# Four graph neural network layers on one core: the lags of the attention jobs in a planner's order of priorities, for the last graphs

## The chip, the cores and the metric

The kernel runs on one core of a Trainium2 chip. The metric is the device time of one execution in microseconds (us). The core's engines are named as in the profile: PE (TensorE, matmuls), PEld (its weight loads), DVE (VectorE), ACT (ScalarE), POOL (GpSimd) and SP (SyncE, which here only issues DMAs).

## The reference

There are 16 graphs of 1024 nodes with 128 features each; `adj` holds one 1024 x 1024 matrix of zeros and ones per graph. Four layers follow one another, each on the layernorm and relu of x and with x added to its result:

```python
h = relu(layernorm(x)); x = x + sage3(h, dilate(adj), ...)      # layer 0: three convolutions, batch norms over all graphs
h = relu(layernorm(x)); x = x + attention(h, adj, ...)          # layer 1
h = relu(layernorm(x)); x = x + gat(h, adj, W, a)               # layer 2
h = relu(layernorm(x)); x = x + gcn(h, adj, W, b)               # layer 3
# layer 1: 4 heads of 32; softmax(q k^T * 32**-0.5 + log(max(adj, 1e-8))) @ v, then @ Wo.T + bo
# layer 2: e[i,j] = leaky_relu(s_i[i] + s_j[j], 0.2) where adj > 1e-8; softmax over i, 4 heads; alpha^T @ (h @ W)
# layer 3: D^-1/2 (adj + I) D^-1/2 h @ W.T + b,   D = row sums of adj + I
```

Layer 0 needs statistics over all graphs. Layers 1 to 3 need only their own graph, so graph 5 can be in layer 3 while graph 7 is in layer 1.

## The kernel before

`whole` runs layer 0 first (`dilate_plain`, `convolutions_plain`, up to about 1580 us of the profile) and then `attentions_plain`, in which the change lies. This function does layers 1 to 3 of all graphs in one stretch. It consists of seven generators, the jobs, each of which loops over the 16 graphs:

- `matrices` brings the rows of A (fp8) of a graph, checks that A is symmetric (L1318 to L1335: ACT, DVE, PE), and ends with `dinv` (DVE L1338, POOL L1340). Only then is `A[b]` there for the others.
- `before` finishes layer 0 for a graph (L1365), makes the norm (L1265 to L1282, output `h_a`), q, k and v.
- `attend` makes 16 tiles per graph: ACT writes a scaled piece of A over a PSUM tile of four banks (L1416, out `t`), PE adds k^T q to it (L1421, eight matmuls), ACT takes two exponentials (L1429, out `e`). There is one PSUM tile and there are two `e` buffers, so tile n waits until `values` has used tile n - 2.
- `values` multiplies each `e` with v and with ones (L1452), divides (L1458, L1460), multiplies with Wo (L1303) and adds to x (L1462). With that the attention of the graph is complete.
- `positive` makes the masks of layer 2 on DVE (L1503, 32 a graph, out `pm`), from scores that go through DRAM (`dst<-scores`).
- `gat` is the rest of layer 2: norm (output `h`), the product with W (L1523), the split in three bf16 parts (L1549 to L1555), sums with A (L1563) and with the masks (L1578), and the closing operations on POOL and DVE (L1587 to L1598).
- `gcn` is layer 3: norm (output `h_g`), parts (L1615 to L1621), the product with A (L1632, L1636), the product with W (L1303), the last additions on POOL (L1610, L1644), and the store.

A job's generator works on one graph at a time, so gat of graph 15 can't begin ahead of the end of gat of graph 14. `matrices` and `before` of graph b wait until gcn of graph b - 4 and the attention of graph b - 2 are done (four buffers for A and x). Jobs other than `attend` and `values` share two PSUM banks, the pool "sum".

No engine chooses at run time: every engine gets one list of instructions, in the order in which the planner `in_order` lets the generators go on. Each `yield` announces the next operation: engine, planned duration, the planned time from which its inputs are there, and the change in PSUM banks. The planner takes the job with the smallest key, gives it its operation and a planned end, and goes on. The key has three parts:

```python
start = max([free[engine], needs] + [min(pools[pool]) for pool, change in tiles(j) if change > 0])
key = (start, engine == "PE", j["did"] / j["per"] + j["lag"])
```

`did` is the planned PE time that the job has had so far and `per` a number from the list at L1649, so `did / per` is a progress, roughly in graphs. A small key is a high priority. The planned durations are constants, and the chip's differ from them. The planner is also used at L921, for layer 0, with lags that are plain numbers.

Of the kernel before, what the change touches and what calls it, by code (L numbers as in the profile page):

```python
# [1213 lines left out]
def attentions_plain(tc, x, spill, final, ready_weights, adj, deg, trouble, eye, out, scores, bound, reach):  # L1214
    nc = tc.nc
    with ExitStack() as ctx:
# [26 lines left out]
        def bank(pool=psg, name="sum"):  # L1243
            return pool.tile([P, HN], F32, name=name)
# [63 lines left out]
        def matrices():  # L1308

            for b in range(B):  # L1310
                while done["gcn"] < b - 3 or done["attend"] < b - 1:
                    yield
                m = adp.tile([P, NB, N], F8, name="A")
                for i in range(NB):
                    t = yield "ACT", 1.3, 0.0, 0
                    a = lp.tile([P, N], F32, name="a")
                    nc.sync.dma_start(a, adj[b, i * P:(i + 1) * P, :])
                    nc.scalar.activation(m[:, i, :], a, AF.Relu, accum_out=deg[:, b, i:i + 1], saturate=False)  # L1318
                    yield "DVE", 1.4, 0.0, 0
                    junk = lp.tile([P, N], F8, name="junk", bufs=1)  # L1320

                    nc.vector.scalar_tensor_tensor(junk, a, 0.0, a, op0=ALU.is_gt, op1=ALU.not_equal,
                                                   accum_out=trouble[:, b, i, 0:1], saturate=False)
                    for hf in range(2):
                        w = min(HN, (i - 4 * hf) * P)
                        if w > 0:
                            e = yield "PE", 0.1 + w / 1024, t, 1
                            ps = bank()
                            nc.tensor.matmul(ps[:, :w], ident16, m[:, i, hf * HN:hf * HN + w], start=True, stop=False)
                            for j in range(w // P):  # L1330
                                nc.tensor.matmul(ps[:, j * P:(j + 1) * P], m[:, 4 * hf + j, i * P:(i + 1) * P], minus16,
                                                 start=False, stop=j == w // P - 1)
                            yield "ACT", 0.8, e, -1
                            junk = lp.tile([P, HN], BF16, name="junk2", bufs=1)
                            nc.scalar.activation(junk[:, :w], ps[:, :w], AF.Abs, accum_out=trouble[:, b, i, 1 + hf:2 + hf])  # L1335

                t = yield "DVE", 0.2, 0.0, 0
                nc.vector.tensor_scalar(dinv[:, b], deg[:, b], 1.0, None, op0=ALU.add)  # L1338
                yield "POOL", 1.7, t, 0
                nc.gpsimd.tensor_tensor(dinv[:, b], dinv[:, b], minus_half, op=ALU.pow)  # L1340
                A[b] = m
# [55 lines left out]
        def attend():  # L1397

            last = 0.0


            s = pss.tile([P, H, HN], F32, name="t")
            for hd in range(H):
                for c in range(4):
                    nc.tensor.matmul(s[:, hd, c * P:(c + 1) * P], ident16, ident16, start=c == 0, stop=c == 3)
            n = 0
            for b in range(B):
                while b not in ready or b not in A:
                    yield
                t, xt, qT, kT, va = ready[b]  # L1410
                for hf in range(2):
                    cols = slice(hf * HN, (hf + 1) * HN)
                    for k in range(NB):
                        e = yield "ACT", 1.9, last, 0

                        nc.scalar.activation(s, A[b][:, k, None, cols].to_broadcast([P, H, HN]), AF.Copy, scale=16.0)  # L1416
                        e = yield "PE", 1.1, max(e, t), 0

                        for hd in range(H):
                            r = slice(hd * HD, (hd + 1) * HD)  # L1420
                            nc.tensor.matmul(s[:, hd], kT[r, k * P:(k + 1) * P], qT[r, cols], start=False, stop=True,  # L1421
                                             skip_group_check=True)
                        while n > 1 and n - 2 not in taken:
                            yield
                        es = ep.tile([P, H, HN], F32, name="e")
                        e = max(e, taken.get(n - 2, 0.0))
                        for hd in range(0, H, 2):
                            e = yield "ACT", 1.07, e, 0
                            nc.scalar.activation(es[:, hd:hd + 2], s[:, hd:hd + 2], AF.Exp, scale=SIGMA)  # L1429
                        exps[n] = es, e  # L1430
                        last = e
                        n += 1
# [213 lines left out]
                done["gcn"] += 1  # L1646

        with tc.manual_schedule(engines=set(ENGINES.values())):
            in_order([(0, 4.0, matrices()), (3, 18.0, before()), (0.5, 17.6, attend()), (3, 34.0, values()), (1, 2.0, positive()),  # L1649
                      (1, 54.0, gat()), (2.5, 17.0, gcn())], {"sum": 2})  # L1650


ENGINES = {"PE": mybir.EngineType.PE, "ACT": mybir.EngineType.Activation, "DVE": mybir.EngineType.DVE,
           "POOL": mybir.EngineType.Pool}
HOP = 0.25


def in_order(jobs, pools):

    free = dict.fromkeys(ENGINES, 0.0)
    pools = {name: [0.0] * n for name, n in pools.items()}
    first = next(iter(pools))
    jobs = [{"lag": lag, "per": per, "job": job, "next": next(job), "held": {}, "did": 0.0, "asked": False}
            for lag, per, job in jobs]

    def tiles(j):  # L1670
        bank = j["next"][3]
        return bank if isinstance(bank, list) else [bank if isinstance(bank, tuple) else (first, bank)]

    while True:
        best = None
        for j in jobs:
            while j["next"] is None and not j["asked"]:
                j["next"], j["asked"] = next(j["job"], "end"), True
            if j["next"] in (None, "end"):
                continue  # L1680
            engine, took, needs, _ = j["next"]
            start = max([free[engine], needs] + [min(pools[pool]) for pool, change in tiles(j) if change > 0])
            key = (start, engine == "PE", j["did"] / j["per"] + j["lag"])
            if best is None or key < best[0]:
                best = (key, start, j)
        jobs = [j for j in jobs if j["next"] != "end"]
        if best is None:
            assert not jobs
            break
        _, start, j = best  # L1690
        assert start < float("inf")
        engine, took, needs, _ = j["next"]
        end = free[engine] = start + took
        if engine == "PE":
            j["did"] += took
        for pool, change in tiles(j):
            if change > 0:
                k = pools[pool].index(min(pools[pool]))
                pools[pool][k] = float("inf")
                j["held"].setdefault(pool, []).append(k)  # L1700
            elif change < 0:
                pools[pool][j["held"][pool].pop(0)] = end + HOP
        try:
            j["next"] = j["job"].send(end + HOP)
        except StopIteration:
            jobs.remove(j)
        for o in jobs:
            o["asked"] = False
# [39 lines left out]
def whole(tc, x, adj, nodemask, chunk_mats, chunk_mask, eye, sel, p, out):  # L1748
    nc = tc.nc
    with tc.tile_pool(name="dram", bufs=1, space=DRAM) as dp, tc.tile_pool(name="keep", bufs=1) as kp:  # L1750
# [19 lines left out]
        with tc.tile_pool(name="final", bufs=1) as fp:  # L1770
            final = [fp.tile([P, D], F32, name=f"final{i}") for i in range(3)] + [fp.tile([3, D], BF16, name="final_row")]
            with tc.tile_pool(name="early", bufs=1) as yp, tc.tile_pool(name="c_adj", bufs=2) as ap, \
                    tc.tile_pool(name="c_x", bufs=2) as xp:
                ident = yp.tile([P, P], F32, name="ident")
                nc.sync.dma_start(ident, eye)
                minus_half = yp.tile([P, NB], F32, name="minus_half")
                nc.vector.memset(minus_half, -0.5)
                h0 = xp.tile([P, NB, D], F32, name="xt")
                attention_weights(tc, ap, ident, ready_weights, *weights)
                dilate_plain(tc, adj, eye, kept, rdeg, unsettled, norm_first(tc, x, yp, h0, minus_half))  # L1780
                convolutions_plain(tc, x, ident, ap, xp, h0, minus_half, kept, rdeg, spill, final, *layer0)
            attentions_plain(tc, x, spill, final, ready_weights, adj, deg, trouble, eye, out, scores, bound, reach)
# [45 lines left out]
```

## Time and profile before

| | |
|---|---|
| time, median of three runs | 3990.11 us (3984.71 to 3998.74) |
| the profiled execution: its time | 3983.57 us |
| its span in the profile | 3981.8 us |
| mean granted PE clock | 0.932 |
| busy in the span: PE / DVE / ACT / POOL | 86% / 63% / 60% / 20% |
| layers 1 to 3 (`attentions_plain`) | from about 1580 us to the end |
| first attention tile / start of the last | 1609.6 us / 3825.5 us |

Attention's 16 tiles of a graph took between 102.9 and 169.9 us from the first L1416 to the next graph's first, and 119.1 us up to the last L1416 in graph 15.

How to read what follows: a window table gives the busy time of each engine within a stretch; a timeline gives instructions in order of their start, merged where alike, and in brackets how long the engine was idle before it and which instruction is taken to have released it. Where a helper such as the norm serves several jobs, the output's name (`h_a`, `h`, `h_g`) tells which job it is.

### The profile page before, as it was taken

What the parts mean: (1) busy time and instruction counts of PE and PEld (TensorE: products, weight loads), DVE (VectorE), ACT (ScalarE), POOL (GpSimd) and SP (SyncE); (2) the same over time, 40 slices, a digit from 0 to 9 for tenths busy, and PEclk for the clock granted to TensorE, in tenths of its full rate; (3) what the DMA queues carried; (4) which work ended last, traced back from release to release, by engine and by line L of the source; (5) the groups of instructions that cost most, each with busy time, mean ns of one, the idle gap of its engine ahead of it and who ended that gap; (6) DMA issues with size and microseconds to landing.
All of it is one profiled execution on the core that took longest, in us unless ns stands there. A gap on an engine that the chain in (4) does not pass through costs nothing.

```text
span 3981.8 us, 65726 instructions
## 1 busy us (share of the span) xinstructions
PE 3429.2 (86%) x26692; PEld 1966.6 (49%) x26692; DVE 2528.4 (63%) x4782; ACT 2398.6 (60%) x3961; POOL 790.9 (20%) x680
## 2 busy tenths in 40 slices
PE   4888887899999986789899898998989899889775
PEld 2556565445555565335554544544444454454333
DVE  4988784553344444247775777677687686777656
ACT  3778764453333345776677676767757767776540
POOL 6545421210010011102121111111111101210110
PEclk9989986999999997999999998998999989999887
DMA  9632223443333314211221122122122112111000
GB/s 107 41 21 16 12 79 122 160 170 122 127 128 129 129 61 141 79 59 49 65 86 59 49 75 76 37 75 79 41 67 81 48 50 85 56 58 49 27 17 17
DMA packets 182499, 293.20 MB, mean 74 GB/s; under 512 B 77468, under 2 KB 124456, under 8 KB 173992
## 3 DMA queue, kind: packets, MB, share of 16 engines
q1 hardware_dynamic: 91944, 221.69, 17.1%
q0 software_dynamic: 79728, 24.66, 7.6%
q10 hardware_dynamic: 10512, 42.54, 2.7%
q8 instruction: 211, 3.46, 0.4%
q14 instruction: 104, 0.85, 0.1%
HBM read 287.98 MB, written 51.19 MB: 85 GB/s over the span
## 4 chain that ended last, share of the span: by engine, by line
PE 60%; DVE 20%; ACT 8%; DMA 5%; issue 3%; POOL 3%; ACTq 0%; SPq 0%; POOLq 0%; DVEq 0%
PE g L1040 12%; PE acc L1452 10%; PE sum L1578 9%; PE t L1421 5%; PE sum L1632 4%; PE sum L1563 4%; DVE pm L1503 3%; DMA rows<-in_adj_dram 2%; DVE rows L882 2%; PE sum L1365 2%; PE o L1089 2%; DVE r L835 2%; PE o L1090 2%; ACT e L1429 1%; PE sum L1383 1%
## 5 line engine op out<-in xcount | busy, mean ns | idle before, releaser
L1429 ACT ACTIVATE e<-t 128x1024 f32<-128x1024 f32 x512 | 507.9, 1022 | 485.8 <-PE t L1421 467.9
L1503 DVE SCALAR_TENSOR_TENSOR pm<-dst,minus,A 128x1024 fp8e4<-128x1024 f32 x512 | 675.5, 1348 | 8.4 <-DMA dst<-scores 8.3
L1040 PE MATMUL g<-C,parts 128*128 128x512 fp8e4 x2304 | 523.9, 382 | 15.9 <-DVE aggT L1042 10.0
L1416 ACT ACTIVATE t<-A 128x2048 f32<-128x2048 fp8e4 x256 | 482.0, 1883 | 3.9 <-ACT dst L1483 0.3
L1578 PEld LDWEIGHTS <-pm 128*128 128x128 fp8e4 x4096 | 346.6, 98 | 187.0 <-issue 165.0
L1578 PE MATMUL sum<-parts,pm 128*128 128x198 bf16 x4096 | 399.7, 251 | 26.1 <-DVE pm L1503 16.4
L1452 PE MATMUL acc<-e,va 128*32 128x512 f32 x2048 | 331.6, 620 | 41.1 <-ACT e L1429 38.2
L1040 PEld LDWEIGHTS <-parts 128*128 128x128 bf16 x2304 | 224.0, 99 | 264.1 <-issue 9.6
L1421 PE MATMUL t<-qT,kT 32*128 32x512 f32 x2048 | 303.5, 663 | 30.6 <-ACT t L1416 30.3
L1452 PE MATMUL acc<-e,ones_hd 128*32 128x512 f32 x2048 | 318.4, 599 | 0.0
L1581 DVE TENSOR_REDUCE pos<-sum 128x132 f32<-128x396 f32 x256 | 144.8, 566 | 201.1 <-PE sum L1578 200.5
L1563 PE MATMUL sum<-parts,A 128*128 128x396 bf16 x1024 | 212.1, 352 | 44.9 <-DVE parts L1555 24.0
L1042 DVE TENSOR_TENSOR aggT<-g,rdb 128x512 f32<-128x512 f32 x96 | 66.1, 690 | 270.6 <-PE g L1040 270.5
L1632 PE MATMUL sum<-A,gparts 128*128 128x512 fp8e4 x768 | 176.3, 382 | 24.9 <-ACT gparts L1615 17.6
L1045 POOL TENSOR_TENSOR nrm<-nrm,minus_half 128x8 f32<-128x8 f32 x48 | 78.6, 1638 | 594.3 <-DVE nrm L1103 585.9
L835 DVE TENSOR_TENSOR r<-ya,both 128x512 bf16<-128x512 f16 x184 | 140.4, 777 | 87.9 <-ACT ya L832 87.0
L1275 POOL TENSOR_TENSOR ln_st<-ln_st,minus_half 128x8 f32<-128x8 f32 x48 | 86.1, 1794 | 510.5 <-DVE ln_st L1273 348.4
L1563 PEld LDWEIGHTS <-A 128*128 128x128 fp8e4 x1024 | 94.7, 99 | 183.7 <-issue 106.6
L882 DVE SCALAR_TENSOR_TENSOR rows<-y,thirty,rows 128x1024 fp8e4<-128x1024 f16 x128 | 168.5, 1324 | 24.0 <-ACT y L874 23.5
L1100 ACT ACTIVATE sq<-o 128x512 f32<-128x512 f32 x96 | 55.2, 596 | 204.7 <-PE o L1093 125.1
L872 PE MATMUL big<-tri,rows 128*128 128x256 fp8e4 (+3 forms) x896 | 175.6, 318 | 0.6 <-ACT y L874 0.4
L885 POOL TENSOR_TENSOR own<-rows,lower 128x256 bf16<-128x256 fp8e4 x128 | 109.1, 862 | 334.2 <-DVE rows L882 201.2
(291 smaller groups left out, 6779.7 us busy)
## 6 DMA issues: line engine op xcount, KB each, us to landing
a<-in_adj_dram SPq DMA_DIRECT2D x128, 512.0 KB
C<-kept SPq DMA_DIRECT2D x48, 1024.0 KB
dst<-scores SPq DMA_DIRECT2D x64, 512.0 KB
rdb<-rdeg SPq DMA_DIRECT2D x48, 512.0 KB
spill<-hT ACTq DMA_DIRECT2D x48, 512.0 KB
kept<-rows ACTq DMA_DIRECT2D x16, 1024.0 KB
h_a<-spill SPq DMA_DIRECT2D x64, 256.0 KB
hT_a<-spill SPq DMA_DIRECT2D x16, 512.0 KB
```

Source lines behind the costliest of these rows:

```text
L835: nc.vector.tensor_tensor(r, ya, both[:, 1, :, None].to_broadcast([P, G, P]), op=ALU.is_equal)
L872: nc.tensor.matmul(ps[:, k * P:], lhs, triF[:, :HN - k * P], start=k == 0, stop=k == 3)
L882: nc.vector.scalar_tensor_tensor(row, y16, hh[:, g:g + 1], row, op0=ALU.not_equal, op1=ALU.mult, saturate=False)
L1040: nc.tensor.matmul(ps, parts[:, k, j, :], C[:, j, cols], start=j == 0 and k == 0, stop=j == NB - 1 and k == 2)
L1416: nc.scalar.activation(s, A[b][:, k, None, cols].to_broadcast([P, H, HN]), AF.Copy, scale=16.0)
L1421: nc.tensor.matmul(s[:, hd], kT[r, k * P:(k + 1) * P], qT[r, cols], start=False, stop=True, skip_group_check=True)
L1429: nc.scalar.activation(es[:, hd:hd + 2], s[:, hd:hd + 2], AF.Exp, scale=SIGMA)
L1452: nc.tensor.matmul(ps[r], ones if one else va[:, k, r], es[:, hd], start=k == 0, stop=k == NB - 1)
L1503: nc.vector.scalar_tensor_tensor(pm[:, i, :], dst[hd], minus[:, i, hd:hd + 1], A[b][:, i, :], op0=ALU.is_ge, op1=ALU.mult, saturate=False)
L1563: nc.tensor.matmul(ps[:, :3 * H * W], A[b][:, i, j * P:(j + 1) * P], parts4[:, i, :, :, W:], start=i == 0, stop=i == NB - 1)
L1578: nc.tensor.matmul(ps[:, jj * 6 * W:(jj + 1) * 6 * W], pm[:, i, (j + jj) * P:(j + jj + 1) * P], flat(parts4[:, i, hd]), start=i == 0, stop ...
L1632: nc.tensor.matmul(ps, parts[:, k, m, :], A[b][:, m, cols], start=m == 0 and k == 0, stop=False)
```

## The change

The lag of four jobs becomes a pair. The first number holds as before; once the job's `did / per` is above LATE = 12.5, the second holds instead. For `matrices`, `before`, `attend` and `values` the second is 2 less than the first. `positive`, `gat` and `gcn` keep their lags. Nothing else is different: the same operations, buffers, DMAs and planned durations.

```diff
-            in_order([(0, 4.0, matrices()), (3, 18.0, before()), (0.5, 17.6, attend()), (3, 34.0, values()), (1, 2.0, positive()),
+            in_order([((0, -2), 4.0, matrices()), ((3, 1), 18.0, before()), ((0.5, -1.5), 17.6, attend()), ((3, 1), 34.0, values()), (1, 2.0, positive()),
                       (1, 54.0, gat()), (2.5, 17.0, gcn())], {"sum": 2})
...
 HOP = 0.25
+LATE = 12.5
...
-            key = (start, engine == "PE", j["did"] / j["per"] + j["lag"])
+            key = (start, engine == "PE", j["did"] / j["per"] + (j["lag"] if not isinstance(j["lag"], tuple) else j["lag"][j["did"] / j["per"] > LATE]))
```

## The prediction

> **What bounds the kernel now.** I read the page first, then the stretch of the span from graph 12 on by stages, then the engines' timelines at the end. The page:
>
> ```profile
> span 3981.8 us, 65726 instructions
> PE 3429.2 (86%) x26692; PEld 1966.6 (49%) x26692; DVE 2528.4 (63%) x4782; ACT 2398.6 (60%) x3961; POOL 790.9 (20%) x680
> PE   4888887899999986789899898998989899889775
> ACT  3778764453333345776677676767757767776540
> PEclk9989986999999997999999998998999989999887
> ```
>
> In the part that the change can reach (from 1580 us on), TensorE is busy nine tenths in nearly every slice, and only the last two slices fall to 7 and 5. So work order can win little in the middle and something at the end. Busy time by stage of the end (columns: window, length, then busy us and instruction count of PE, PEld, DVE, ACT, POOL, then the granted clock, DMA share, GB/s):
>
> ```profile
> 3694.00:3816.00 122.00, 104.30 (x768) 51.47 (x770) 80.17 (x110) 70.72 (x76) 17.06 (x10) 0.91 0.07 22
> 3816.00:3848.00 32.00, 26.26 (x166) 12.03 (x158) 13.06 (x29) 13.40 (x20) 4.00 (x2) 0.89 0.00 1
> 3848.00:3875.00 27.00, 8.57 (x30) 5.09 (x31) 12.93 (x29) 10.93 (x19) 8.06 (x6) 0.66 0.20 60
> 3875.00:3943.00 68.00, 45.10 (x320) 33.65 (x319) 56.49 (x61) 0.00 (x0) 3.06 (x1) 0.78 0.05 16
> 3943.00:3982.00 39.00, 16.17 (x88) 8.30 (x88) 8.99 (x23) 6.62 (x14) 6.32 (x3) 0.68 0.06 17
> ```
>
> The stages are: gat of graph 14 (its last DVE operation, L1598, ends at 3816), the rest of attention 15 (its result x, L1462, is complete at 3848), then gat 15 (to 3943) and gcn 15 (to 3982). Gat 15 needs x of graph 15, and its generator is free from 3816. **So 3848 - 3816 = 32 us of the end are a wait for attention 15**, and the 134 us after it are a chain that the change does not shorten. In its first 27 us TensorE does only 8.57 us of work. Who makes attention 15 late is in the timelines of ACT and of PE (start, length, engine, line):
>
> ```profile
> 3818.62 1.02 ACT L1429 ACTIVATE e<-t 128x1024 f32<-128x1024 f32 x1 [1.32 <-PE t L1421]
> 3821.01 3.18 ACT L1282 ACTIVATE h_g<-x,ln_st 128x128 f32<-128x128 f32 x8 [1.36 <-DVE ln_st L1279]
> 3824.10 1.00 ACT L1429 ACTIVATE e<-t 128x1024 f32<-128x1024 f32 x1
> ```
>
> ```profile
> 3828.72 1.47 PE L1421 MATMUL t<-qT,kT 32*128 32x512 f32 x8
> 3830.12 5.35 PE L1632 MATMUL sum<-A,gparts 128*128 128x512 fp8e4 x24
> 3835.31 0.83 PE L1636 MATMUL sum<-ident,gparts 128*128 128x128 bf16 x12
> 3836.07 1.07 PE L1452 MATMUL acc<-e,va 128*32 128x512 f32 x8
> ...
> 3854.66 3.17 PE L1291 MATMUL sum<-ident,h 128*128 128x128 f32 x8 [6.80 <-ACT h L1282]
> ```
>
> The two exponentials of one attention tile stand 4.5 us apart because the norm of gcn 14 (h_g) was put between them, and the last values of attention 15 (L1452 at 3836) stand behind 6.2 us of gcn 14 (L1632, L1636). Gcn 14 is not urgent: it would fit into the hole before and after 3854.
>
> A second thing costs attention time in these graphs. Between graph 14's last tile (starts 3670.7) and graph 15's first (3706.4) lie 35.7 us, where a tile usually takes about 7:
>
> ```profile
> 3699.72 3.18 ACT L1282 ACTIVATE h_g<-x,ln_st 128x128 f32<-128x128 f32 x8 [16.75 <-DVE dinv L1338]
> 3703.34 3.16 PE L1291 MATMUL sum<-ident,h 128*128 128x128 f32 x8 [17.19 <-ACT h L1282]
> ```
>
> The first tile stands on ACT behind both norms after gat 13, and both engines are empty for 17 us. The planner could not place it sooner because A of graph 15 counts as built only after its dinv step (L1338), and that stands on DVE behind those norms (3699.54).
>
> **What the Trainium skill says.** "PSUM — Partial Sum Buffer", section "Engine vs sequencer instructions": the queues of ACT, DVE and POOL are strictly first in, first out, and matmuls keep program order. The trace agrees: the tile above waits behind norms that it does not need. "Perfetto Trace Analysis", section "Optimization Strategy": where the limit changes by regime, interleaving the regimes may help; the end table shows such a regime. "TensorE: Matmul & The Clock Gate", section "What's actually happening": an idle window of about 3.4 us halves the clock. The trace agrees in kind: 0.66 granted in the thin stage, and eight QK matmuls took 2.09 us after the 17 us hole against 1.14 us before it.
>
> **The change part by part.** No instruction, DMA or buffer is added or removed; only the third part of the planner's key changes. The first is the start time, the second favours engines other than PE, so lags decide only among operations that could start at the same planned time. A job's progress is its planned PE time over `per`. Summing the yields gives the planned PE time of one graph, and over `per` the progress: matrices 4.5/4.0 = 1.125, before 16.1/18 = 0.894, attend 17.6/17.6 = 1, values 33.3/34 = 0.979, positive 2/2 = 1, gat 38.4/54 = 0.711, gcn 14.5/17 = 0.853. So 12.5 is passed in graph 11 by matrices, halfway through graph 12 by attend, in graph 12 by values, and only from graph 14 by before. With attention in the middle of graph 14 the keys are:
>
> - kernel before: gat 10.6, gcn 13.2, positive 14 to 15, attend 15.0, before 16.9, values 17.1, matrices 17.4;
> - after: gat 10.6, attend 13.0, gcn 13.2, before 14.9, values 15.1, matrices 15.4, with positive still 14 to 15.
>
> Hence: **attend passes gcn and positive, narrowly; nobody passes gat; values and matrices stay behind gcn.**
>
> 1. Attend ahead of gcn. I lined up the timelines of ACT and PE: for each tile, what of gcn ran between the moment its next operation was free to go and its start. In graph 13: 5.6 us on PE (L1632, L1636), 3.1 of norm, about 1.0 of casts, 9.8 in all. Graph 14: 3.8, 3.1, 1.1, so 8.0. Graph 15 (gcn 13 and 14): 5.4, 3.1, 2.0, so 10.5. The sum, 28 us, is the upper bound. How much is had depends on the keys when each gcn begins: gcn 11 stands at 0.853 x 11 + 2.5 = 11.9, attend at 13.0 - 1.5 = 11.5, so attend leads for six tiles: all of 9.8. Gcn 12 (12.74) meets attend at tile 2 (12.62), which leads for two tiles: half, 4. Gcn 13 (13.59) meets tile 0 (13.5), gcn 14 (14.44) tile 14 (14.38): again two tiles each: half, 5. Together 19 us.
> 2. Given back. Values stay behind gcn on PE, and attend can be only two tiles ahead of them (two e buffers). PE was 128.84 us busy in the 140 us of graph 13, so part of what attend wins comes back as waiting for values: I take 3, between 0 and 19.
> 3. Gcn later. Its displaced work (14 us on PE, 7 on ACT, per graph) is covered by the hole of gat 15, where PE has 27 - 8.57 = 18 us free. If that cover fails, a gcn piece of 6.2 us stands in front of gat 15: I take 0, at most 6. The gate of graph 15's loads is gcn 11, done at about 3465, while its first load is used at 3552: 87 us to spare.
> 4. Matrices, before and values against positive: near ties on DVE (1.23 against 1.35 us an operation). Eight loads of 512 KB for a matrix and six for x and the spilled layers are issued on SP with these steps, and may now precede a dst load there; the masks (L1503) waited 8.3 us for dst in the whole run. I take 0, from -4 to +4. POOL's queue has the same steps, 12% busy in that stretch.
> 5. The hole of 17 us: dinv remains behind gat (10.6) and gcn (13.2), so I leave it where it is. If it goes, about 15 us more.
>
> Sum: 19 - 3 = 16 us, capped by the 32 us after which gat 14 is the later of the two. The profiled execution took 3983.57 us (span 3981.8, 1.8 around it), 6.5 below the median 3990.11. So a like execution should take 3967.6, and against the median 3974.
>
> **The rivals.**
>
> - *Attention gets on by more*: the hole of 17 us goes too, or two holes merge. Then x 15 is there when gat 14 ends, gain 30 to 40 (gat 14 itself gets shorter without company): 3955. For it: 35.7 us between two tiles is the largest gap. Against: dinv's key is the last of all, before and after. 0.15.
> - *No effect*: values, not attend, set the pace, PE being nine tenths busy, and only the last two tiles gain (4.5 us of norm). 3985, and also the result if equal start times are too rare for lags to matter. 0.20.
> - *Slower*: the new plan puts a graph boundary of graph 13 or 14 behind the norms like that one. Place: the first L1416 of a graph on ACT. Price: graph 14 with such a hole took 169.1 us, graph 13 without 140.5; 28.6, of which graph 15 (126 us to its end) won back 10, so 19. It decides once the gain of steps 1 and 2 is under 7; with 3 of it left, 4006. For it: the trace has four such gaps (35 to 38 us, after graphs 2, 5, 9, 14), so a new plan can draw one. Against: only three boundaries are replanned. 0.16.
>
> **How the numbers follow.** My forecast has 0.49. A difference under 0.3% (12 us) is about what a measurement of this kernel cannot tell from no change. The forecast's 16 us is near that edge; its bounds are 9 to 30, and I give 0.02 of it to "within". Faster 0.47 + 0.15 = 0.62; within 0.20 + 0.02 = 0.22; slower 0.16. The range goes from 3945 (the hole gone and gat 14 shorter) to 4004, leaving out most of the slower case.
>
> **What the changed profile would show.** Right: L1416's last start before 3815 instead of 3825.5; the last x (L1462) 10 to 25 us before 3848; L1632 of gcn 14 inside 3830 to 3875, after the last L1452; gat 15 to the end still about 134 us. Gcn 12 and 13 later than their norms allow. Step 2 wrong: attend waiting for L1452. Step 5 wrong: no gap over 15 us before the first L1416 of graph 15. I am wrong altogether if gat 14 ends after x 15, or if the stretch after x 15 grows by more than 6 us.

## The result, and the profile after

The changed kernel takes 3964.3 us (median of 7), the kernel before 3987.8 (7): a ratio of 0.9948, interval 0.9933 to 0.9964, so 14 to 27 us faster. The forecast was 3974, a gain of 16 on the 3990 that were known then. The number held, though 3964 lies as near to the first rival's 3955. **The account behind it did not**: the sign that was named for being wrong altogether, gat 14 ending after x of graph 15, is there.

The page of the profile after:

```profile
span 3970.3 us, 65722 instructions
PE 3426.2 (86%) x26692; PEld 1966.5 (50%) x26692; DVE 2521.8 (64%) x4782; ACT 2397.1 (60%) x3961; POOL 797.4 (20%) x680
PE   4888887899999987788989987998998989998875
ACT  3778764453333345786677676667666767767630
PEclk9999986999999998899999998999998999999987
```

The work is the same; the slices of the middle differ by a tenth here and there, and at the end 9775 has become 8875. This execution took 3972.1 us, one of three near 3973 (three others lie at 3960.3), so its profile shows less than the median gain. Its layer 0 and first graphs were also some us later: attention 12 begins at 3265.1 instead of 3260.6. From there on the two profiles can be set against each other: 721.2 us to the end before, 705.1 after, 16.1 less.

The windows of the end, cut at the same events as before (gat 13 ends, x 15 is complete, gat 14 ends, first L1563 of gat 15, gat 15 ends):

```profile
3714.00:3816.00 102.00, 89.58 (x655) 45.48 (x656) 74.21 (x103) 56.55 (x65) 13.30 (x8) 0.96 0.08 27
3816.00:3831.00 15.00, 5.79 (x57) 5.39 (x55) 11.19 (x14) 0.00 (x0) 3.06 (x1) 0.73 0.00 0
3831.00:3864.00 33.00, 24.02 (x109) 12.80 (x110) 19.07 (x49) 16.97 (x33) 10.21 (x7) 0.68 0.11 33
3864.00:3932.00 68.00, 44.05 (x331) 34.29 (x329) 58.48 (x63) 0.00 (x0) 6.31 (x2) 0.84 0.08 24
3932.00:3970.00 38.00, 16.26 (x88) 8.33 (x88) 8.17 (x21) 6.62 (x14) 6.31 (x3) 0.68 0.06 17
```

The second row is the reverse of before. There x 15 came 31.4 us after the end of gat 14 (32 in the prediction's rounded windows). Now it comes 14.6 us ahead of it, and in between ACT is empty. Counted from the start of attention 12 (3260.6 and 3265.1):

| | before | after | difference |
|---|---|---|---|
| x of graph 15 complete | 587.0 | 551.2 | -35.8 |
| gat 14 ends | 555.6 | 565.8 | +10.2 |
| so gat 15 can begin | 587.0 | 565.8 | -21.2 |
| gat 15 | 95.9 | 100.7 | +4.8 |
| gcn 15 to the end | 38.4 | 38.7 | +0.3 |

Attention gained more than the whole sum of the prediction, and gat lost some of it again. The largest single gain of attention is on ACT's timeline at the boundary from graph 14 to 15:

```profile
3663.30 1.90 ACT L1416 ACTIVATE t<-A 128x2048 f32<-128x2048 fp8e4 x1
...
3674.99 0.49 ACT L1335 ACTIVATE junk<-sum 128x384 bf16<-128x384 f32 x1 [4.50 <-PE sum L1331]
...
3675.47 1.87 ACT L1416 ACTIVATE t<-A 128x2048 f32<-128x2048 fp8e4 x1
...
3719.23 3.18 ACT L1282 ACTIVATE h<-x,ln_st 128x128 f32<-128x128 f32 x8 [1.27 <-DVE ln_st L1279]
```

The first tile of graph 15 follows the last symmetry check of A (L1335) at once, 12.2 us after the tile before it instead of 35.7. The norms after gat 13 come only at 3719. These 23.5 us are not all: the boundaries after graphs 12 and 13 lost 15.6 us (14.3 and 13.6 us between two tiles instead of 6.0 and 6.3), and within the graphs attention gained 27.9, most of it in graph 13, where the time from the first tile to the last fell from 134.3 to 113.0 us.

Where gat lost: gat 11 to 12 took 153 us (L1598 to L1598) instead of 136, while gat 13 and 14 took 140 and 117 instead of 141 and 122. In gat 12 it is the second score copy of positive (L1483) that moved. First before, then after:

```profile
3448.83 0.57 ACT L1483 COPY dst<-sum 4x512 f32<-4x512 f32 x1
...
3455.51 0.57 ACT L1483 COPY dst<-sum 4x512 f32<-4x512 f32 x1
```

```profile
3458.07 0.56 ACT L1483 COPY dst<-sum 4x512 f32<-4x512 f32 x1
...
3479.17 0.56 ACT L1483 COPY dst<-sum 4x512 f32<-4x512 f32 x1
```

The two halves lay 6.7 us apart and now lie 21.1 apart. Counted from the end of gat 11 (3417 and 3421.5), the second copy moved from 38.5 to 57.7 us, the first mask from 45.5 to 65.2.

Gat 15 lost its 5 us in the third window row, mainly on ACT and PE:

```profile
3839.01 3.17 ACT L1282 ACTIVATE h_g<-x,ln_st 128x128 f32<-128x128 f32 x8
3842.08 1.04 ACT L1293 COPY hT<-sum 128x512 f32<-128x512 f32 x2
...
3847.45 3.58 PE L1481 MATMUL sum<-hT,weights 128*4 128x512 f32 x4
...
3850.98 5.83 PE L1632 MATMUL sum<-A,gparts 128*128 128x512 fp8e4 x24
...
3857.32 5.34 PE L1632 MATMUL sum<-A,gparts 128*128 128x512 fp8e4 x24
...
3864.11 1.57 PE L1563 MATMUL sum<-parts,A 128*128 128x396 bf16 x8
```

Gcn 14 stands in the hole of gat 15, as forecast, but is not free there. Its norm (`h_g`) stands ahead of the copies that gat 15 needs (L1293), and its products (L1632) ahead of L1563, whose parts were ready at 3862.4. L1563 begins 33.2 us after gat 15 could, instead of 27.9. In the kernel before, the products of gcn 14 were done before gat 15 could begin.

### The profile page after: what moved, and what is told of

It is laid out like the page before. It is cut to its first block, busy times and chain, and to the rows that moved or that the text cites. A ratio compares the mean times of both kernels' runs of the same rounds, so it can differ in the third digit from the quotient of the medians.

```text
span 3970.3 us, 65722 instructions
## 1 busy us (share of the span) xinstructions
PE 3426.2 (86%) x26692; PEld 1966.5 (50%) x26692; DVE 2521.8 (64%) x4782; ACT 2397.1 (60%) x3961; POOL 797.4 (20%) x680
## 4 chain that ended last, share of the span: by engine, by line
PE 57%; DVE 16%; ACT 7%; issue 3%; DMA 3%; POOL 2%; ACTq 0%; SPq 0%; POOLq 0%; DVEq 0%
PE g L1040 12%; PE acc L1452 9%; PE sum L1578 9%; PE t L1421 5%; PE sum L1632 4%; DVE pm L1503 3%; PE sum L1563 3%; PE sum L1365 2%; PE o L1089 2%; PE o L1090 2%; DVE rden L1458 1%; PE sum L1383 1%; ACT e L1429 1%; PE sum L1303 1%; PE t L1029 1%
## 5 line engine op out<-in xcount | busy, mean ns | idle before, releaser
L1416 ACT ACTIVATE t<-A 128x2048 f32<-128x2048 fp8e4 x256 | 481.9, 1882 | 3.6
L1563 PE MATMUL sum<-parts,A 128*128 128x396 bf16 x1024 | 207.0, 346 | 28.3 <-DVE tot L1566 21.4
L1632 PE MATMUL sum<-A,gparts 128*128 128x512 fp8e4 x768 | 179.0, 386 | 24.7 <-ACT gparts L1615 17.7
L882 DVE SCALAR_TENSOR_TENSOR rows<-y,thirty,rows 128x1024 fp8e4<-128x1024 f16 x128 | 169.4, 1331 | 24.1 <-ACT y L874 23.5
L1322 DVE SCALAR_TENSOR_TENSOR junk<-a 128x1024 fp8e4<-128x1024 f32 x128 | 160.5, 1254 | 24.6 <-DMA a<-in_adj_dram 24.3
L1563 PEld LDWEIGHTS <-A 128*128 128x128 fp8e4 x1024 | 93.1, 97 | 166.3 <-issue 92.4
```

The source lines that it names most:

```text
L882: nc.vector.scalar_tensor_tensor(row, y16, hh[:, g:g + 1], row, op0=ALU.not_equal, op1=ALU.mult, saturate=False)
L1563: nc.tensor.matmul(ps[:, :3 * H * W], A[b][:, i, j * P:(j + 1) * P], parts4[:, i, :, :, W:], start=i == 0, stop=i == NB - 1)
L1632: nc.tensor.matmul(ps, parts[:, k, m, :], A[b][:, m, cols], start=m == 0 and k == 0, stop=False)
```

## The experiments

Theory A is the prediction's step 1: attend passing gcn is the gain. Theory B: the three jobs that feed attention and empty its buffers bring it, above all an A that is ready sooner. Theory C: what gat lost comes from positive being passed. Theory D: the gap at the boundary is the late moment at which A counts as ready. All ratios are to the kernel before.

**1. Attend's late lag alone, and everything but it.**

```diff
 # e1_attend_alone, against the changed kernel
-in_order([((0, -2), 4.0, matrices()), ((3, 1), 18.0, before()), ((0.5, -1.5), 17.6, attend()), ((3, 1), 34.0, values()), ...
+in_order([(0, 4.0, matrices()), (3, 18.0, before()), ((0.5, -1.5), 17.6, attend()), (3, 34.0, values()), ...
 # e2_without_attend
+in_order([((0, -2), 4.0, matrices()), ((3, 1), 18.0, before()), (0.5, 17.6, attend()), ((3, 1), 34.0, values()), ...
```

> Only attend has the late lag (0.5, then -1.5); matrices, before and values keep theirs. Theory A, the prediction's step 1 (attend passing gcn is the gain): nearly the whole difference, a ratio of 0.995 to before, near 3967 us. Theory B (the gain comes from the three jobs that feed attention and empty its buffers, the lead of attend itself mostly pushes back the score step of positive, L1481 and L1483): under 8 us, 3980 to 3990, with a late L1483 and a gat of 150 us in one of the graphs 12 to 14.

Measured: 0.9989 (0.9977 to 1.0000), about 4 us, and 7.2 us in the profile from attention 12 on. As the account of the gain, theory A falls. But attend's lag brings attention as far forward as steps 1 and 2 said: x of graph 15 is complete after 566.3 us, counted as above, instead of 587.0, and the tiles of graph 13 take 122.6 us from first to last instead of 134.3. Part of that is taken back at once, since attention, being ahead, now waits for the next A. A gap of 24.4 us lies at the boundary to graph 14, whose first tile stands directly behind the last check of its A:

```profile
3542.88 0.49 ACT L1335 ACTIVATE junk<-sum 128x384 bf16<-128x384 f32 x1 [0.64 <-PE sum L1331]
...
3543.36 1.87 ACT L1416 ACTIVATE t<-A 128x2048 f32<-128x2048 fp8e4 x1
```

A gap of 27.3 us stays at the boundary to graph 15, and gat 13 takes 156 us instead of 141. Most of the 20.7 us by which x 15 is sooner is lost only after x 15: gat 15 takes 109.3 us instead of 95.9. On PE, gcn 14 stands ahead of the score products of graph 15 (L1481), which precede it in the changed kernel:

```profile
3843.23 5.34 PE L1632 MATMUL sum<-A,gparts 128*128 128x512 fp8e4 x24
...
3849.18 1.02 PE L1481 MATMUL sum<-hT,weights 128*4 128x512 f32 x2
...
3856.08 1.02 PE L1481 MATMUL sum<-hT,weights 128*4 128x512 f32 x2
```

The first mask follows 39.3 us after gat 15 can begin, against 26.7 in the changed kernel.

> The mirror image: matrices, before and values have their late lags, attend keeps 0.5. Theory A: the gain is gone, ratio 0.999 to 1.001. Theory B: the gain stays and grows, because attend no longer precedes positive: gat 12 takes 136 to 145 us again instead of 152, which is worth up to 16 us more; ratio 0.988 to 0.993, 3940 to 3960 us.

Measured: 0.9923 (0.9909 to 0.9937), some 31 us. The gain is there without attend's late lag, and larger than with it, though the intervals just touch. Gat 12 took 138 us. The windows of the end:

```profile
3696.00:3809.00 113.00, 102.24 (x782) 52.31 (x778) 80.65 (x110) 66.26 (x73) 16.05 (x9) 0.95 0.07 24
3809.00:3814.00 5.00, 0.00 (x0) 0.00 (x0) 4.90 (x6) 0.00 (x0) 0.00 (x0) 0.50 0.00 0
```

Here x 15 is complete 4 us ahead of the end of gat 14. Gat 14 ends 555.6 us after the start of attention 12 (3258.6), as before, so the whole wait of 31.4 us is gone. The sum closes: 31.4, less 4.9 for the longer gat 15, is 26.5; this profile's stretch from attention 12 to the end is 26.6 us shorter (694.6 against 721.2). X 15 comes 35.4 us sooner here and 35.8 in the changed kernel: next to the other three lags, attend's adds nothing to it.

**2. Matrices alone.**

```diff
 # e3_matrices_alone, against the changed kernel
+in_order([((0, -2), 4.0, matrices()), (3, 18.0, before()), (0.5, 17.6, attend()), (3, 34.0, values()), ...
```

> Only matrices has the late lag (0, then -2). If the gap of 35.7 us at the boundary from graph 14 to 15 comes from A being built last of all, this alone closes it: no gap over 15 us before the first L1416 of graph 15, and 15 to 25 us are gained (ratio 0.994 to 0.996). If attention's progress needs values or attend to be earlier, it gains under 8 us. Theory A: nothing.

Measured: 0.9939 (0.9919 to 0.9958), some 24 us. The gap at the last boundary is 7.7 us; the last row of A of graph 15 has been read at 3629 instead of 3674. One lag of the four does what all four together do.

**3. Where A counts as ready.** This is the kernel before with all its lags; one line is moved.

```diff
 # e5_A_before_dinv, against the kernel before
+                A[b] = m
                 t = yield "DVE", 0.2, 0.0, 0
                 nc.vector.tensor_scalar(dinv[:, b], deg[:, b], 1.0, None, op0=ALU.add)
                 yield "POOL", 1.7, t, 0
                 nc.gpsimd.tensor_tensor(dinv[:, b], dinv[:, b], minus_half, op=ALU.pow)
-                A[b] = m
```

> The kernel before, with all lags as they were; only the line that declares A of a graph ready stands ahead of the dinv step (which layer 3 alone needs) instead of after it. Theory D, that the gap of 35.7 us at the boundary from graph 14 to 15 comes from A being declared ready only after dinv has had its turn on DVE behind two norms: the gap goes, attention 15 begins 20 to 25 us sooner, x of graph 15 is there when gat 14 ends, and the time falls by 15 to 20 us to a ratio near 0.9955, as much as the whole change. If the gap was only a sign of attention being late anyway, the ratio stays within 0.998 to 1.001.

Measured: 0.9964 (0.9951 to 0.9976), some 14 us, a little under what was expected. ACT at the boundary:

```profile
3687.42 0.49 ACT L1335 ACTIVATE junk<-sum 128x384 bf16<-128x384 f32 x1 [4.75 <-PE sum L1331]
...
3687.90 1.87 ACT L1416 ACTIVATE t<-A 128x2048 f32<-128x2048 fp8e4 x1
```

and the dinv step on DVE (L1339 here, by the moved line) is as late as it was:

```profile
3704.64 0.16 DVE L1339 TENSOR_SCALAR dinv<-degree 128x8 f32<-128x8 f32 x1
```

So dinv still waits behind the norms, but attention does not wait for it: 12.1 us between the tiles instead of 35.7. That is theory D, and it shows that the gap was a cause and not a sign. The last 16 tiles took 112.2 us here against 119.1. X 15 comes 29.9 us sooner in all, of which gat 15 takes 11.5 back (107.4 us instead of 95.9).

**4. Gcn later, and nothing else.**

```diff
 # e6_gcn_later, against the kernel before; the third number is this job's own LATE
-                      (1, 54.0, gat()), (2.5, 17.0, gcn())], {"sum": 2})
+                      (1, 54.0, gat()), ((2.5, 4.5, 9.3), 17.0, gcn())], {"sum": 2})
```

> The kernel before, with all attention jobs and positive as they were; gcn alone gets a lag higher by 2 from graph 11 on (2.5, then 4.5, above a progress of 9.3), so that attend passes gcn and nothing else changes. Theory A (step 1, with its 28 us of gcn work in front of attention tiles): 10 to 19 us, ratio 0.995 to 0.9975. Theory B: within 5 us, ratio 0.9985 to 1.001, because the values stay behind the masks' sums and the matrices, and a gap over 20 us remains at one of the last three boundaries.

Measured: 1.0022 (1.0008 to 1.0035), slower by 3 to 14 us. The slowdown is the prediction's slower rival, so the run does not test theory A alone. Attention does gain by passing gcn: the tiles of graph 13 take 118.8 us from first to last, and x 15 comes 14 us sooner. But the boundary from graph 13 to 14 drew a gap of 48.9 us (6.3 before), behind the norm of gat 13, with ACT empty for 18 us:

```profile
3546.95 0.49 ACT L1335 ACTIVATE junk<-sum 128x384 bf16<-128x384 f32 x1 [2.30 <-PE sum L1331]
...
3565.62 3.18 ACT L1282 ACTIVATE h<-x,ln_st 128x128 f32<-128x128 f32 x8 [18.09 <-DVE ln_st L1279]
3568.71 1.86 ACT L1416 ACTIVATE t<-A 128x2048 f32<-128x2048 fp8e4 x1
```

So x 14 was late, and gat 14 with it, which ends 28 us later than in the kernel before.

**5. Positive's place.** First the changed kernel with positive lowered too, then a lead of 3 instead of 2 without attend's.

```diff
 # e4_positive_too, against the changed kernel
-..., (1, 2.0, positive()),
+..., ((1, -1, 11.9), 2.0, positive()),
 # e8_lead_of_3
+in_order([((0, -3), 4.0, matrices()), ((3, 0), 18.0, before()), (0.5, 17.6, attend()), ((3, 0), 34.0, values()), (1, 2.0, positive()),
```

> The changed kernel, and positive also gets 2 less from graph 12 on (1, then -1, from a progress of 11.9). Theory C, that the 16 us by which gat 12 is longer (152 against 136) come from positive's second score copy standing 19 us later behind the attention jobs: gat 12 returns to about 140 us, and as gat 14 was the later of the two at the end, the end moves by up to 15 us: 3950 to 3958. If gat 12 was long because its matmuls shared PE with more attention work, it stays at 150 us and the time at 3964.

Measured: 0.9936 (0.9922 to 0.9951). Gat 12 took 131 us, and the second score copy came at 3458.87, 6.4 us after the first. Theory C holds for gat 12. In time the run can't be told from the changed kernel, as the intervals overlap: attention lost part of its lead (gaps of 22.8 and 17.5 us at the boundaries to graphs 14 and 15), and x 15 is again the later one, at 3820 against 3811.

> As the run without attend's late lag, but matrices, before and values lead by 3 in place of 2, so that in each of the last graphs they pass positive clearly and not in a near tie. Theory C (an attention job that passes positive sets back its score step, and with it the masks and gat): L1483 more than 25 us later after its norm than in the kernel before, gat of graphs 12 and 13 at 155 us or more, the gain gone and 10 to 30 us lost: ratio 1.002 to 1.008. If positive's place does not matter, the ratio is that of the lead of 2, 0.992.

Measured: 1.0025 (1.0015 to 1.0035), slower by 6 to 14 us. The gap at the boundary to graph 15 is gone (6.6 us), yet from gat 11 to gat 12 it took 156 us and then 152. In gat 12 the second copy came 33 us after the first:

```profile
3461.22 0.57 ACT L1483 COPY dst<-sum 4x512 f32<-4x512 f32 x1
3494.24 0.56 ACT L1483 COPY dst<-sum 4x512 f32<-4x512 f32 x1
```

So the same lead that removes the gap can cost more than it brings. A limit stays open: from the first score values on DVE (L1527) to the second copy it took 37.8 us in gat 12 of the changed kernel and 39.2 in gat 13 of e2, but the former gat took 153 us and the latter 143. Above 47 us (four graphs, in e1 and e8) gat took 152 to 156 every time. What hides 39 us in one graph and not in another was not separated.

**6. A better version.** As e2, with LATE = 11.0.

```diff
 # e7_no_attend_late11, against the changed kernel
+in_order([((0, -2), 4.0, matrices()), ((3, 1), 18.0, before()), (0.5, 17.6, attend()), ((3, 1), 34.0, values()), (1, 2.0, positive()),
...
-LATE = 12.5
+LATE = 11.0
```

> As the run without attend's late lag, and LATE = 11.0 in place of 12.5, so that matrices takes its lead in graph 9 to 10 and before and values in graphs 11 to 12. Theory B: matrices that are built sooner at two boundaries more (10 to 11 and 11 to 12) give a few us beyond the run without attend's late lag: ratio 0.989 to 0.992. If only the last boundary counts, it is the same as that run, 0.992 to 0.993.

Measured: 3944.5 us, 0.9906 (0.9884 to 0.9927), the fastest of all (four executions); its interval lies just below that of the changed kernel. The gain over e2 (0.9923) is within the intervals. In its profile a second long gap is gone too, the one after graph 9 (38 us before): attention 11 begins at 3107.5 instead of 3121.5, while the gaps after graphs 2 and 5 lie ahead of any late lag.

**All runs at the same events.** Times in us, one profile each, counted from the start of attention 12. The tiles of graph 13 are taken from the first L1416 to the last. Gat 15 can begin at the later of x 15 and the end of gat 14, and is counted from there.

| | tiles of graph 13 | gap after 13 | gap after 14 | x 15 complete | gat 14 ends | gat 15 |
|---|---|---|---|---|---|---|
| before | 134.3 | 6.3 | 35.7 | 587.0 | 555.6 | 95.9 |
| changed | 113.0 | 13.6 | 12.2 | 551.2 | 565.8 | 100.7 |
| e1, attend alone | 122.6 | 24.4 | 27.3 | 566.3 | 565.7 | 109.3 |
| e2, without attend | 131.4 | 12.8 | 5.8 | 551.5 | 555.6 | 100.8 |
| e3, matrices alone | 135.1 | 7.3 | 7.7 | 546.0 | 541.8 | 106.8 |
| e4, positive too | 122.2 | 22.8 | 17.5 | 557.8 | 548.3 | 106.9 |
| e5, A before dinv | 134.3 | 6.3 | 12.1 | 557.1 | 552.8 | 107.4 |
| e6, gcn later | 118.8 | 48.9 | 7.0 | 572.7 | 583.9 | 99.5 |
| e7, LATE 11.0 | 130.8 | 12.8 | 5.8 | 547.8 | 551.8 | 100.8 |
| e8, lead of 3 | 133.2 | 6.7 | 6.6 | 582.5 | 578.2 | 108.8 |

Two things stand out. In the four kernels in which attend passes gcn (changed, e1, e4, e6), graph 13 takes 113 to 123 us, and in the others 131 to 135; the same four have the longest gaps after it, 13.6 to 48.9 us against at most 12.8. And once gcn 14 falls into gat 15, gat 15 takes 99 to 101 us where gat 14 is the later one, and 107 to 109 where x 15 is. In e1 the score products stand behind gcn 14 and the masks come later; that this is the cause is a reading of the trace, as no run changed that order alone.

## Why the prediction was right in number and wrong in account

- *The number* agreed by luck. The sum had x 15 sooner by 16 us and everything after it unchanged. In the profile x 15 was sooner by 35.8 us, but gat 14 ended 10.2 later and became the later one, and the rest grew by 5: 16.1 us in all. Errors of opposite sign cancelled.
- *The reading of the end* was right. The wait for x 15 is what could be won (31.4 us, not 32), and e2 wins just this wait. That the chain after it is not shortened holds too, but it grew in every run.
- *Steps 1 and 2* (attend ahead of gcn, 19 us, less 3) were right in sum about attention, though not graph by graph, and wrong about the end. By attend's lag alone x 15 comes 20.7 us sooner, yet the time falls by about 4 us (e1). In the change the other three lags bring x 15 forward as far without it (e2). How much came back as waiting for values, step 2's term, was not measured; in e1 attention waited for the next A.
- *Step 3* (gcn 14 in the hole, 0, at most 6) was at its bound in the change and mis-sized beyond it. With gcn 14 in it, gat 15 took 5 us longer in the changed kernel and in e2, but 11 to 13 in e1, e3, e4, e5 and e8. This is why e1 keeps so little. The step counted free time on PE and not the order in which gat's own operations and the scores of graph 15 come to stand with gcn 14.
- *Step 4* priced the wrong passing. It looked at near ties of matrices, before and values with the mask operations on DVE, from -4 to +4. The list of keys says that attend passes positive, and no step gave that a price. It cost 17 us in gat 12, in the score step on PE and ACT: without attend's lag gat 12 takes 138 us (e2), with positive lowered too 131 (e4), against 153. (POOL was busy for 15% of the stretch from attention 12 on, not 12%.)
- *Step 5* (the gap of 35.7 us stays) failed by its own sign: 12.2 us are left. It argued that dinv's key is last both before and after, which is true, and concluded that the gap stays. But the gap needs two things at one time: A just finished, and the norms after gat in front of dinv. Whatever pulls the two apart removes it: matrices earlier (e3), A declared sooner (e5), or attention ahead of gat and gat later, as in the changed kernel. The value put on it, about 15 us, agrees with the 14 that e5 measured, but as a difference of two terms that the prediction did not have: 29.9 us sooner at x 15, 11.5 lost in gat 15.
- *The rivals*: the first (the gap goes too, x 15 is there when gat 14 ends, 3955) has the mechanism nearest to what happened, with the difference that gat came later: gat 14 itself did get shorter (117 us from 122), but gat 12 had taken 17 us more. E2 has both the rival's mechanism and its time (3953). The slower rival did not happen in the change but is real: e6 drew such a gap (graph 13 took 167.8 us instead of 140.5, the 27 us of the prediction's price before any is won back).

From the Trainium skill, "PSUM — Partial Sum Buffer", section "Engine vs sequencer instructions" (strict order in an engine's queue), the argument of the gap stands: 16.75 us of an empty ACT in the kernel before, 18.09 in e6. The section "Optimization Strategy" of "Perfetto Trace Analysis" (mix the regimes) holds with a price: the thin stage of gat 15, up to L1563, took in gcn 14 and grew by 5 us.

## What to carry to other kernels

When a planner's list fixes the order, look first for the moments at which all engines are empty behind a wait that nobody needs, and ask what condition made the planner put it there: one line that declared A ready before an unrelated step was worth 14 us, most of what the four lags brought. Don't end a sum at an event that is not the end: attend's lag alone brought x 15 forward by 21 us and the end by about 4, because what came after grew. Test one lag at a time, since here one of the four was enough, and with another one left out the kernel was, if anything, faster. And a job that is passed must be followed to those who wait for it, on every engine, even where it has only 2 us of work.

## What was not expected of the hardware

The executions of the changed kernel fall in two groups, 3960.3 to 3960.4 us (three) and 3972.1 to 3973.3 (three), with one at 3964.3, at mean granted clocks of 0.938 to 0.939, 0.934 to 0.935 and 0.937. Seven executions do not show whether the groups are more than chance, and their cause is open. Differences of 10 us between kernels therefore need several executions or an alignment of the profiles at a common event, as done above.
